# Scattering eight raw fields of an edge instead of a full row of 143 values, in a graph network of four layers

## The chip, the cores and the metric

The kernel runs on one core of a Trainium2 chip. The time is that of the whole program on the device, in microseconds. A run of the profiler takes one execution apart; times inside it are counted from the start of its span. The engines are named as in the profile: PE multiplies matrices (PEld loads its weights), DVE is the vector engine, ACT the scalar engine, POOL the general engine that also issues the indirect transfers, and SP only issues transfers. Each works through its own queue of instructions in order.

## The reference, cut to what matters

A graph of 3,125 nodes with 32 features and 103,125 edges (50,000 pairs in both directions and one loop per node). Four layers are added to the features one after the other: attention with four heads, a mean over neighbours in two steps, a Gaussian mixture, and a spline convolution on positions that a small network with two further spline convolutions moves. The part that the change touches belongs to the edges: every edge has its two ends and five attributes. Three of these are a position `pseudo` in [0, 1], from which the splines take a cell and weights:

```python
def spline_basis(pseudo):
    pos = pseudo * (KS - 1)
    i0 = jnp.clip(jnp.floor(pos), 0, KS - 2).astype(jnp.int32)
    frac = pos - i0
    basis = jnp.prod(jnp.where(combos[None] == 1, frac[:, None, :], 1.0 - frac[:, None, :]), axis=-1)
    idx = jnp.sum((i0[:, None, :] + combos[None]) * strides[None, None, :], axis=-1)
    return (basis, idx)

def spline_conv(x, row, col, basis, idx, W, b):
    z = jnp.einsum('ni,kio->nko', x, W).reshape(N * K, Fout)
    gathered = z[col[:, None] * K + idx]
    msg = jnp.einsum('es,eso->eo', basis, gathered)
    out = jax.ops.segment_sum(msg, row, num_segments=N)
    deg = jax.ops.segment_sum(jnp.ones_like(msg[:, 0]), row, num_segments=N)
    return out / jnp.maximum(deg, 1.0)[:, None] + b
```

with KS = 5, so 125 kernel positions and 8 corners per edge. For the first of the spline convolutions the input feature is 1 for every node, so only the sums of the 125 basis values over the edges of a node are needed.

## The kernel before

**Stages.** The nodes are held in 25 chunks of 128. The work goes through these stages, with their times in the profiled execution:

- *Places* (0 to 132 us, `places_of_edges`). For each edge the place in a table is found: edges with the same source chunk are packed into tiles of 128, 855 tiles in all. Eight fields of an edge (low part of the source, target, three Gaussian weights, three position values) are collected in `flds`, field by field, and stored to `fields_d` (L1036 to L1144).
- *Scatter* (132 to 1,832 us, L1544 to L1706). `put_edges` (L1564) takes 26 columns of 128 edges at a time: SP loads their fields (L1567), DVE computes cells, the eight corner weights and all 125 basis values into `pay` (L1570 to L1593, three buffers), and POOL sends 26 indirect transfers (L1595), each of 128 rows of 143 values (`ROW` = 17 + 125 + 1; 572 bytes) into the table `tab` in device memory. There are 31 such blocks, 806 transfers. Rows that may remain empty are filled by transfers on ACT's queue first (L1562).
- Inside the scatter stage the tiles are read back by groups. A group is 2 to 5 units of 24 tiles (one tile per full source chunk), and five small groups of 3 tiles hold the last chunk. `add_tiles` (L1623) loads the rows of three source chunks at a time (L1637, on SP), copies the ends (DVE, L1643) and the 17 narrow values (ACT, L1646), and then goes source chunk by source chunk: DVE makes one-hots of the source (L1650, helper L1374), PE multiplies them with the 126 wide values of the rows (L1653), and the sum is added to `sums` (L1608). For groups that come early enough (`counted`) the same step also counts edges between nodes: ACT casts the one-hots (L1657), DVE makes one-hots of the targets (`od`, L1381), PE multiplies (L1496), DVE or ACT takes the counts on (L1520, L1522), and `counts_out` (L1530) stores the counts, their transpose and a third array, `off`, which is 0 where an edge exists and very large elsewhere (ACT, L1534; `a_off` has one buffer).
- *Spline convolution 2* (1,832 to about 3,760 us). Per chunk PE computes the table `z` (L1445), ACT and DVE copy it to slabs, ACT's queue stores them. `summed_rows` (L1708) then gathers, tile by tile (POOL, L1731), multiplies by corner weights (DVE, L1735) and sums with one-hots (PE, L1736). The corner weights of a group come into `w8` (L1890). Beside it, in portions that `beside` deals out, run the remaining counts and the maximum of the attention scores (L1836 to L1843): SP loads `off` for each source chunk and third of the targets, and DVE runs one subtract-and-maximum per head (L1841).
- *Attention* (to 4,685), the mean, the mixture and the new positions (to 5,755), and the *last spline convolution* (5,755 to 7,187), which has the same shape as the earlier one at half the width, with 12 gather buffers, three buffers for `prod` and two for the one-hots `oh2`.

**The order.** The order of the program around the scatter is written by hand: after each block, steps of the groups whose tiles are complete are put in, two blocks late (`LAG`, L1683 to L1697), so that they spread over the blocks until the next group comes. A group can be read when the blocks up to its `need` have been scattered: 71, 155, 292, 425, 557, 689, 768, 806 and 806 columns for the nine large groups. The last three large groups (72, 96 and 72 tiles) and two small ones are worked off after the last block (L1699 to L1705), two at a time in turn. What reads `tab` has been declared independent of the scatters of later blocks (L1639), so only the scatters of earlier blocks are waited for.

Of the kernel before, what the change touches and what calls it, by code (L numbers as in the profile page):

```python
# [8 lines left out]
F32 = mybir.dt.float32  # L9
BF = mybir.dt.bfloat16  # L10
I32 = mybir.dt.int32
I16 = mybir.dt.int16
AF = mybir.ActivationFunctionType
OP = mybir.AluOpType
# [4 lines left out]
P = 128  # L19
# [855 lines left out]
ROW = NAR + K3 + 1  # L875
# [101 lines left out]
def places_of_edges(tc, a, pl, tr, fields_d, slot_d):  # L977
# [12 lines left out]
    with tc.tile_pool(name="bk", bufs=1) as pool:  # L990
# [45 lines left out]
        flds = pool.tile([P, 8, tr], F32, name="flds")  # L1036
# [107 lines left out]
        nc.sync.dma_start(fields_d, flds.rearrange("p f t -> p (f t)"))  # L1144
# [42 lines left out]
def cells(nc, pool, pos, n):  # L1187

    cell = pool.tile([P, 3, n], F32, name="cell")
    tmp = pool.tile([P, 3, n], F32, name="cell_t")  # L1190
    nc.vector.tensor_scalar(cell, pos, 1.0, None, op0=OP.is_ge)
    for k in range(2, KS - 1):
        nc.vector.tensor_scalar(tmp, pos, float(k), None, op0=OP.is_ge)
        nc.vector.tensor_add(cell, cell, tmp)
    hat = pool.tile([P, 3, 2, n], F32, name="hat")
    nc.vector.tensor_sub(hat[:, :, 1, :], pos, cell)
    nc.vector.tensor_scalar(hat[:, :, 0, :], hat[:, :, 1, :], -1.0, 1.0, op0=OP.mult, op1=OP.add)
    return cell, hat


def corner_weights(nc, pool, cell, hat, n, w8, row):

    w4 = pool.tile([P, 2, 2, n], F32, name="w4")
    nc.vector.tensor_mul(w4, hat[:, 1, :, None, :].to_broadcast([P, 2, 2, n]),
                         hat[:, 2, None, :, :].to_broadcast([P, 2, 2, n]))
    nc.vector.tensor_mul(w8, w4.rearrange("p j k t -> p (j k) t")[:, :, None, :].to_broadcast([P, 4, 2, n]),
                         hat[:, 0, None, :, :].to_broadcast([P, 4, 2, n]))
    tmp = pool.tile([P, n], F32, name="cell_row")
    nc.vector.scalar_tensor_tensor(tmp, cell[:, 0], float(KS), cell[:, 1], op0=OP.mult, op1=OP.add)
    nc.vector.scalar_tensor_tensor(row, tmp, float(KS), cell[:, 2], op0=OP.mult, op1=OP.add)  # L1210
# [3 lines left out]
def tile_gnn_places(ctx: ExitStack, tc: tile.TileContext, a: dict, out: bass.AP, pl, fields_d, slot_d):  # L1214
# [34 lines left out]
    big = const.tile([P, 1], F32, name="big")  # L1249
    nc.vector.memset(big, BIG)  # L1250
# [60 lines left out]
    off_d = [dram.tile([P, NPAD], BF, name=f"off_d{s}") for s in range(NCH)]  # L1311
# [170 lines left out]
    def count_edges(g, s, oh, cps, tps):  # L1482
# [9 lines left out]
        for i, (t, w) in enumerate(tiles):  # L1492
            od = cn_a.tile([P, 9 * P], BF, name="od3", bufs=4)
# [9 lines left out]
    def add_counts(s, cols, cn, tps):  # L1503

        lo, width = cols[0][0], len(cols)
        a_s = cn_a.tile([P, 8 * P], F16, name="a_s")
# [23 lines left out]
    def counts_out(s, lo, n, a_s, tps):  # L1530

        nc.sync.dma_start(as_d[s][:, lo * P : (lo + n) * P], a_s[:, : n * P])
        off = cn_a.tile([P, 8 * P], BF, name="a_off", bufs=1)
        nc.scalar.activation(off[:, : n * P], a_s[:, : n * P], AF.Relu, bias=big, scale=-BIG)  # L1534
        nc.sync.dma_start(off_d[s][:, lo * P : (lo + n) * P], off[:, : n * P])
        a_t = cn_a.tile([P, 8 * P], F16, name="a_t")
# [7 lines left out]
    SB = 3  # L1544
    assert S % SB == 0
    GK = max(len(g.units) for g in pl.groups)
    GT = max(g.n for g in pl.groups)
    with tc.tile_pool(name="ed", bufs=1) as once, tc.tile_pool(name="ed_pay", bufs=3) as pays, \
            tc.tile_pool(name="ed_s", bufs=2) as small_p, tc.tile_pool(name="s1", bufs=2) as pool, \
# [5 lines left out]
        EM = 5  # L1555
# [8 lines left out]
        def put_edges(t0):  # L1564
            n = BLK
            at = small_p.tile([P, 8, BLK], F32, name="flds", bufs=3)
            nc.sync.dma_start(at, fields_d.rearrange("p (f t) -> p f t", f=8)[:, :, t0 : t0 + n])  # L1567
            pay = pays.tile([P, BLK, ROW], F32, name="pay")
            pos = small_p.tile([P, 3, BLK], F32, name="pos")
            nc.vector.tensor_scalar(pos, at[:, 5:8], float(KS - 1), None, op0=OP.mult)  # L1570
            cell, hat = cells(nc, small_p, pos, n)
            nc.vector.tensor_copy(pay[:, :, 0:8].rearrange("p t f -> p f t"), at)
            corner_weights(nc, small_p, cell, hat, n, pay[:, :, 9:17].rearrange("p t (c i) -> p c i t", i=2), pay[:, :, 8])
            w15 = small_p.tile([P, 3, KS, BLK], F32, name="w15")
            tmp = small_p.tile([P, 3, BLK], F32, name="w15_t")
            for k in range(KS):
                if k < KS - 1:
                    nc.vector.scalar_tensor_tensor(w15[:, :, k, :], cell, float(k), hat[:, :, 0, :],
                                                   op0=OP.is_equal, op1=OP.mult)
                if k:  # L1580
                    dest = tmp if k < KS - 1 else w15[:, :, k, :]
                    nc.vector.scalar_tensor_tensor(dest, cell, float(k - 1), hat[:, :, 1, :],
                                                   op0=OP.is_equal, op1=OP.mult)
                    if k < KS - 1:
                        nc.vector.tensor_add(w15[:, :, k, :], w15[:, :, k, :], tmp)
            w25 = small_p.tile([P, KS, KS, BLK], F32, name="w25")
            nc.vector.tensor_mul(w25, w15[:, 0, :, None, :].to_broadcast([P, KS, KS, n]),
                                 w15[:, 1, None, :, :].to_broadcast([P, KS, KS, n]))
            nc.vector.tensor_mul(
                pay[:, :, NAR : NAR + K3].rearrange("p t (i k) -> p i k t", k=KS),  # L1590
                w25.rearrange("p i j t -> p (i j) t")[:, :, None, :].to_broadcast([P, KS * KS, KS, n]),
                w15[:, 2, None, :, :].to_broadcast([P, KS * KS, KS, n]))
            nc.vector.memset(pay[:, :, ROW - 1 :], 1.0)  # L1593
            for k in range(n):
                put = nc.gpsimd.indirect_dma_start(  # L1595
                    out=tab, out_offset=bass.IndirectOffsetOnAxis(ap=slot[:, t0 + k : t0 + k + 1], axis=0),
                    in_=pay[:, k, :], in_offset=None, bounds_check=P * NT - 1, oob_is_err=False)
# [3 lines left out]
                tc.add_to_no_dep_group(f"rows{t0}", put.ins)  # L1601

# [20 lines left out]
        def add_tiles(g, nar, m, s0, ns):  # L1623

            t0, off = g.t0, s0 if ns == SB else 0
            tt = pool.tile([P, GK, SB, ROW], F32, name="tt")
            if ns == SB:
                src = tabv[:, t0 : t0 + g.n, :].rearrange("e (k s) f -> e k (s f)", s=S)[:, :, s0 * ROW : (s0 + ns) * ROW]
                mine = tt[:, :m, :, :]
                into = mine.rearrange("p k s f -> p k (s f)")  # L1630
                spread = lambda v: v.rearrange("p f (k s) -> p f k s", s=S)[:, :, :, s0 : s0 + ns]
            else:
                src = tabv[:, t0 : t0 + m, :].rearrange("e k f -> e (k f)")
                into = tt.rearrange("p k s f -> p (k s f)")[:, : m * ROW]
                mine = into.rearrange("p (k s f) -> p k s f", s=1, f=ROW)
                spread = lambda v: v.rearrange("p f (k s) -> p f k s", s=1)
            got = nc.sync.dma_start(into, src)  # L1637
# [3 lines left out]
            low = spread(ends[:, :, t0 : t0 + g.n])  # L1641
            for f in range(2):
                nc.vector.tensor_copy(low[:, f], mine[:, :, :, f])  # L1643
            nv = spread(nar[:, :, : g.n])
            for k in range(m):
                nc.scalar.copy(nv[:, :, k, :].rearrange("p f s -> p s f"), mine[:, k, :, :NAR])  # L1646
            for i in range(ns):
                s = g.units[0].tiles[s0 + i][0] if ns == SB else S
                oh = pool.tile([P, GK, P], F32, name="oh1")
                onehots(oh, iota_f, low[:, 0, :, i], m)  # L1650
                acc = psa.tile([P, 512], F32, name="acc1")
                for k in range(m):
                    nc.tensor.matmul(acc[:, : K3 + 1], oh[:, k, :], mine[:, k, i, NAR:], start=(k == 0), stop=(k == m - 1))  # L1653
                counts = None
                if g.counted:
                    ohb = cn_a.tile([P, GK, P], BF, name="oh3")
                    nc.scalar.copy(ohb[:, :m], oh[:, :m])  # L1657
# [3 lines left out]

        def group_steps(g):
            n = g.n
            nar = pool.tile([P, NAR, GT], F32, name="nar", bufs=2)
            if g.t0 < pl.tail:
                for s0 in range(0, S, SB):
                    yield from add_tiles(g, nar, len(g.units), s0, SB)
            else:
                yield from add_tiles(g, nar, n, 0, 1)
            nc.sync.dma_start(narrow_d[g.t0].rearrange("p (f t) -> p f t", f=NAR), nar[:, :, :n])  # L1670
            table_rows(pool, g.t0, n, nar[:, 8, :n], GT)
            for q0 in range(0, n, P):
                q = min(P, n - q0)
                lt = pst.tile([P, 2, P], F32, name="lt")
                for i, (row_d, dt) in enumerate(((lorow_d, BF), (dstrow_d, I16))):
                    nc.tensor.transpose(lt[:q, i, :], ends[:, i, g.t0 + q0 : g.t0 + q0 + q], ident)
                    lr = pool.tile([P, P], dt, name=f"lr{i}")
                    nc.scalar.copy(lr[:q], lt[:q, i, :])
                    nc.sync.dma_start(row_d[g.t0 + q0 : g.t0 + q0 + q], lr[:q])
# [4 lines left out]
        todo = [[g.need + LAG * BLK, (S if g.t0 < pl.tail else 1) + 1, group_steps(g)] for g in pl.groups]  # L1684
# [23 lines left out]
    def summed_rows(grp, fout, table, w8_of, total, first, pool, gp, pp, psa, beside=None):  # L1708
# [14 lines left out]
        for s, tiles in grp.sources.items():  # L1723
            n = len(tiles)
            oh = pool.tile([P, GK, P], F32, name="oh2")
# [530 lines left out]
```

## Time and profile before

| | us |
|---|---|
| median of 3 runs | 7,230.65 |
| lowest, highest | 7,201.02, 7,293.86 |
| the profiled execution | 7,211.97 |
| its span | 7,210.2 |

| engine | busy us | share of the span |
|---|---|---|
| PE | 4,521.4 | 63% |
| DVE | 4,517.0 | 63% |
| POOL | 2,847.0 | 39% |
| PEld | 2,281.7 | 32% |
| ACT | 1,673.9 | 23% |

No engine is full over the whole; each stage has its own limit. The page draws that as 40 slices of 180 us, each digit the busy share of a slice in tenths:

```profile
DVE  5334355533575757877798889917998945444444
POOL 0777544460242534565574000000000035567776
DMA  2123344425787987897883434361114478755553
```

The scatter stage is slices 2 to 10 (from the left), with DVE at half and POOL at 4 to 7 tenths; the first spline convolution is slices 11 to 21, where the transfers and DVE come near full; the last one is slices 32 to 40.

The groups of instructions that the change removes, moves or doubles read as follows (busy us and mean ns of one, then the idle time before them and what ended it):

```profile
L1595 POOL DMA_INDIRECT tab<-pay,slot x806 | 884.7, 1098 | 590.0 <-issue 241.1 <-DVE od L1381 180.9 <-DVE a_s L1520 63.6
L1589 DVE TENSOR_TENSOR pay<-w,w 128x3250 f32<-128x3250 f32 x31 | 176.5, 5694 | 2.3 <-DVE cell L1194 1.1 <-DVE cell_t L1193 1.1
L1841 DVE CUSTOM_DVE_ANT_0 junk<-adr,off 128x1024 f32<-128x1024 f32 (+1 forms) x300 | 379.0, 1263 | 40.3 <-ACT adr L1835 38.3
L1534 ACT ACTIVATE a_off<-a_s,big 128x384 bf16<-128x384 f16 (+4 forms) x219 | 131.9, 602 | 294.8 <-DMA off_d<-a_off 139.4 <-DVE a_s L1520 89.5 <-issue 29.0
```

### The profile page before, as it was taken

The numbers are of one execution on the slowest core, as the hardware profiler recorded it, in microseconds if no ns is written. First come the engines' busy times: TensorE is split into PE (matmuls) and PEld (weight loads), VectorE is DVE, ScalarE is ACT, GpSimd is POOL, SyncE is SP. The second block draws the span as 40 slices with busy tenths as digits, with TensorE's granted clock in tenths as the row PEclk, the third lists the DMA queues.
The fourth block names the chain that finished last, engine by engine and source line by source line (L and its number), as shares of the span: only waits on it lengthen the run. The fifth ranks groups of instructions, "written<-read, shape, count | busy, mean of one in ns | idle before, by whom it ended". The sixth has DMA issues, their size and how long they took to land. (4 is left out here: it accounts for less than half of the span.)

```text
span 7210.2 us, 68160 instructions
## 1 busy us (share of the span) xinstructions
PE 4521.4 (63%) x20874; PEld 2281.7 (32%) x20904; DVE 4517.0 (63%) x9289; ACT 1673.9 (23%) x2940; POOL 2847.0 (39%) x2543
## 2 busy tenths in 40 slices
PE   4013244415888878887778877766775489855555
PEld 1012133214332323222222322255664433333333
DVE  5334355533575757877798889917998945444444
ACT  0012133201434232221103778801110012100000
POOL 0777544460242534565574000000000035567776
PEclk5555566657888977788788999976885556566666
DMA  2123344425787987897883434361114478755553
GB/s 97 53 81 97 86 122 121 124 81 135 265 305 266 335 301 269 322 352 267 291 282 108 119 115 126 101 227 53 57 56 161 160 247 297 237 155 157 159 156 82
DMA packets 554782, 1265.69 MB, mean 176 GB/s; under 512 B 273204, under 2 KB 363263, under 8 KB 541478
## 3 DMA queue, kind: packets, MB, share of 16 engines
q0 software_dynamic: 148912, 613.60, 25.7%
q1 hardware_dynamic: 359062, 388.16, 18.3%
q10 hardware_dynamic: 46432, 259.48, 9.2%
q8 instruction: 168, 2.75, 0.2%
q14 instruction: 208, 1.70, 0.1%
HBM read 907.51 MB, written 387.39 MB: 180 GB/s over the span
## 5 line engine op out<-in xcount | busy, mean ns | idle before, releaser
L1731 POOL DMA_INDIRECT g<-z,base x1710 | 1950.1, 1140 | 1741.9 <-DVE prod L1735 421.8
L1736 PE MATMUL acc<-prod,oh 128*128 128x512 f32 (+1 forms) x3420 | 1690.3, 623 | 733.6 <-DVE prod L1735 506.3
L1736 PEld LDWEIGHTS acc<-prod,oh 128*128 128x128 f32 x3420 | 719.1, 237 | 1663.1 <-issue 828.9
L1595 POOL DMA_INDIRECT tab<-pay,slot x806 | 884.7, 1098 | 590.0 <-issue 241.1
L1374 DVE TENSOR_TENSOR oh<-iota_f,ends 128x640 f32<-128x640 f32 (+3 forms) x663 | 444.5, 672 | 693.7 <-remote 409.8
L1381 DVE TENSOR_SCALAR od<-iota_n,ends 128x512 bf16<-128x512 int16 (+5 forms) x1721 | 536.0, 357 | 495.0 <-remote 207.2
L2189 POOL MEMSET g<- 128x448 f32 x5 | 2.1, 474 | 1876.5 <-PE t_ps L2162 1876.5
L1653 PE MATMUL acc<-tt,oh 128*128 128x126 f32 x1710 | 337.7, 359 | 612.3 <-DVE od L1381 248.5
L1735 DVE TENSOR_TENSOR prod<-g,w 128x512 f32<-128x512 f32 x855 | 579.1, 686 | 211.2 <-DMA g<-z,base 183.5
L1997 PE MATMUL acc<-wt,hx 128*33 128x416 f32 (+1 forms) x1600 | 587.8, 516 | 142.6 <-DVE wt L1995 126.5
L1445 PE MATMUL z_ps<-wk,hts 64*128 64x512 f32 (+1 forms) x800 | 479.9, 845 | 65.6 <-ACT slab L1459 36.2
L1653 PEld LDWEIGHTS acc<-tt,oh 128*128 128x128 f32 x1710 | 302.7, 261 | 650.3 <-issue 427.4
L1496 PE MATMUL cn<-od,oh 128*128 128x256 bf16 (+3 forms) x1331 | 304.7, 358 | 234.4 <-DVE od L1381 107.3
L1841 DVE CUSTOM_DVE_ANT_0 junk<-adr,off 128x1024 f32<-128x1024 f32 (+1 forms) x300 | 379.0, 1263 | 40.3 <-ACT adr L1835 38.3
L1459 ACT COPY slab<-z_ps 128x512 f32<-128x512 f32 (+11 forms) x575 | 289.8, 516 | 486.3 <-DVE slab L1457 309.2
L1735 DVE TENSOR_TENSOR prod<-g,w8n 128x256 f32<-128x256 f32 x855 | 333.5, 423 | 107.0 <-PE acc L1736 49.0
L1991 DVE SCALAR_TENSOR_TENSOR low<-rows,bias_d,low 128x1664 f32<-128x1664 f32 (+1 forms) x200 | 369.4, 1882 | 9.5 <-ACT low L1990 9.5
L1995 DVE SCALAR_TENSOR_TENSOR wt<-low,cnt 128x1664 f32<-128x1664 f32 (+1 forms) x200 | 357.5, 1818 | 15.2 <-PE acc L1997 6.8
L1990 ACT ACTIVATE low<-rows,bias_d 128x1664 f32<-128x1664 f32 (+1 forms) x200 | 325.1, 1628 | 133.4 <-DVE wt L1995 103.0
L1997 PEld LDWEIGHTS acc<-wt,hx 128*33 128x33 f32 x1600 | 168.5, 113 | 527.5 <-issue 334.9
L1993 ACT ACTIVATE low<-low 128x1664 f32<-128x1664 f32 (+1 forms) x200 | 307.0, 1537 | 104.4 <-DVE low L1991 104.3
L1539 PE MATMUL cn<-ident_h,a_s 128*128 128x128 f16 x625 | 98.3, 257 | 336.1 <-DVE a_s L1520 142.7
(348 smaller groups left out, 5211.5 us busy)
## 6 DMA issues: line engine op xcount, KB each, us to landing
z<-slab ACTq DMA_DIRECT2D x100, 1600.0 KB
z<-slab ACTq DMA_DIRECT2D x100, 800.0 KB
lob<-lorow_d SPq DMA_DIRECT2D x70, 768.0 KB
cnt<-at_d SPq DMA_DIRECT2D x100, 416.0 KB
cnt<-as_d SPq DMA_DIRECT2D x50, 800.0 KB
cnt<-at_d SPq DMA_DIRECT2D x100, 384.0 KB
tt<-tab SPq DMA_DIRECT2D x32, 1072.5 KB
g<-z,base POOLq DMA_INDIRECT x1710
```

What stands on the lines that cost most here:

```text
L1374: nc.vector.tensor_tensor(dst_tile[:, :n, :], iota[:, None, :].to_broadcast([P, n, P]), lows[:, :, None].to_broadcast([P, n, P]), OP.is_equal)
L1381: nc.vector.tensor_scalar(dst_tile[:, :w], iota_n[:, lo * P : lo * P + w], ends[:, 1, t : t + 1], None, op0=OP.is_equal)
L1445: nc.tensor.matmul(ps[:, k - k0 : k - k0 + n, :].rearrange("p r f -> p (r f)"), vt[g * fin : (g + 1) * fin, :], wk[g * fin : (g + 1) * fin ...
L1595: put = nc.gpsimd.indirect_dma_start(out=tab, out_offset=bass.IndirectOffsetOnAxis(ap=slot[:, t0 + k : t0 + k + 1], axis=0), in_=pay[:, k, ...
L1653: nc.tensor.matmul(acc[:, : K3 + 1], oh[:, k, :], mine[:, k, i, NAR:], start=(k == 0), stop=(k == m - 1))
L1731: nc.gpsimd.indirect_dma_start(out=g, out_offset=None, in_=table[:rows], in_offset=bass.IndirectOffsetOnAxis(ap=base[:, t : t + 1], axis=0 ...
L1735: nc.vector.tensor_mul(prod, corners(g, fout), w8_of(t).to_broadcast([P, 2, 4, fout]))
L1736: nc.tensor.matmul(acc, oh[:, i, :], prod.rearrange("p j c f -> p (j c f)"), start=(i == 0), stop=(i == n - 1))
L1841: nc.vector.tensor_tensor_reduce(junk, adr[:, hd, :], off, 1.0, -BIG, OP.subtract, OP.max, top[:, j, s, hd : hd + 1])
L1991: nc.vector.scalar_tensor_tensor(low, rows[0], bias_d[:, 0, d, hd : hd + 1], low, op0=OP.add, op1=OP.max)
L1995: nc.vector.scalar_tensor_tensor(wt, low, 1.0, cnt, op0=OP.min, op1=OP.mult)
L1997: nc.tensor.matmul(acc[:, i, :q], hx[:, d, :], wt[:, i * q : (i + 1) * q], start=(d == 0), stop=(d == NCH - 1))
```

## The change

The row of an edge in the table is cut to the eight raw fields, 32 bytes (`ROW` = 8). `places_of_edges` stores the fields edge by edge instead of field by field. `put_edges` only issues the scatters, straight from the fields, which are loaded once in two halves. Cells, corner weights and the one-dimensional weights `w15` are computed after a group has been read back, for all its tiles at once; the 125 basis values are computed for each step (the tiles of one source chunk in the group), by `basis`, into one of three buffers whose last column is 1. The load of a group is one transfer. The first step of a group is these computations alone, so a group has one step more than before.

The array `off` is no longer stored. The attention part loads the counts and makes the flag on DVE, in f32, one instruction for each source chunk and third of the targets (75 in all).

Numbers of buffers change in several places: the pool of the scatter steps 2 to 3 and its small tiles 2 to 1; `od3` 4 to 3, `a_s` 2 to 4, `a_t` 2 to 3; `oh2` 2 to 3; `prod` 3 to 4 in the first spline convolution and 3 to 8 in the last; `w8` 2 to 1. Empty rows are filled 48 tiles at a time instead of 5.

The core of the diff (`cells` and `corner_weights` compute as before, with room for the largest group):

```diff
-ROW = NAR + K3 + 1
+ROW = 8
...
-        flds = pool.tile([P, 8, tr], F32, name="flds")
+        flds_e = pool.tile([P, tr, ROW], F32, name="flds")
+        flds = flds_e.rearrange("p t f -> p f t")
...
-        nc.sync.dma_start(fields_d, flds.rearrange("p f t -> p (f t)"))
+        nc.sync.dma_start(fields_d, flds_e.rearrange("p t f -> p (t f)"))
...
-        off = cn_a.tile([P, 8 * P], BF, name="a_off", bufs=1)
-        nc.scalar.activation(off[:, : n * P], a_s[:, : n * P], AF.Relu, bias=big, scale=-BIG)
-        nc.sync.dma_start(off_d[s][:, lo * P : (lo + n) * P], off[:, : n * P])
-        a_t = cn_a.tile([P, 8 * P], F16, name="a_t")
+        a_t = cn_a.tile([P, 8 * P], F16, name="a_t", bufs=3)
...
+        flds = once.tile([P, tr, ROW], F32, name="e_flds")
+        fv = fields_d.rearrange("p (t f) -> p t f", f=ROW)
+        for t0 in range(0, tr, tr // 2):
+            nc.sync.dma_start(flds[:, t0 : t0 + tr // 2, :], fv[:, t0 : t0 + tr // 2, :])
+        EM = 48
...
         def put_edges(t0):
...
-            for k in range(n):
+            for t in range(t0, t0 + BLK):
                 put = nc.gpsimd.indirect_dma_start(
-                    out=tab, out_offset=bass.IndirectOffsetOnAxis(ap=slot[:, t0 + k : t0 + k + 1], axis=0),
-                    in_=pay[:, k, :], in_offset=None, bounds_check=P * NT - 1, oob_is_err=False)
+                    out=tab, out_offset=bass.IndirectOffsetOnAxis(ap=slot[:, t : t + 1], axis=0),
+                    in_=flds[:, t, :], in_offset=None, bounds_check=P * NT - 1, oob_is_err=False)
...
+        spread = [once.tile([P, GK, K3 + 1], F32, name=f"basis{i}") for i in range(3)]
+        def basis(w15, tiles, m):
+            b = spread[at_step[0] % len(spread)]
+            at_step[0] += 1
+            w25 = pool.tile([P, KS, KS, GK], F32, name="w25")
+            nc.vector.tensor_mul(w25[:, :, :, :m], w15[:, 0, :, None, tiles].to_broadcast([P, KS, KS, m]),
+                                 w15[:, 1, None, :, tiles].to_broadcast([P, KS, KS, m]))
+            nc.vector.tensor_mul(
+                b[:, :m, :K3].rearrange("p t (i k) -> p i k t", k=KS),
+                w25[:, :, :, :m].rearrange("p i j t -> p (i j) t")[:, :, None, :].to_broadcast([P, KS * KS, KS, m]),
+                w15[:, 2, None, :, tiles].to_broadcast([P, KS * KS, KS, m]))
+            return b
...
+        def group_steps(g):
+            n, m, t0 = g.n, len(g.units), g.t0
+            regular = t0 < pl.tail
+            tt = group_p.tile([P, GT, ROW], F32, name="tt")
+            got = nc.sync.dma_start(tt[:, :n, :], tabv[:, t0 : t0 + n, :])
...
+            nc.vector.tensor_copy(ends[:, :, t0 : t0 + n].rearrange("p f t -> p t f"), tt[:, :n, :2])
+            nar = group_p.tile([P, NAR, GT], F32, name="nar")
+            nc.scalar.copy(nar[:, :8, :n].rearrange("p f t -> p t f"), tt[:, :n, :])
+            pos = small_p.tile([P, 3, GT], F32, name="pos")[:, :, :n]
+            nc.vector.tensor_scalar(pos, nar[:, 5:8, :n], float(KS - 1), None, op0=OP.mult)
+            cell, hat = cells(nc, small_p, pos, n, GT)
+            corner_weights(nc, small_p, cell, hat, n, nar[:, 9:17, :n].rearrange("p (c i) t -> p c i t", i=2), nar[:, 8, :n], GT)
+            w15 = group_p.tile([P, 3, KS, GT], F32, name="w15")
...
+            yield
+            for i in range(S if regular else 1):
...
                 oh = pool.tile([P, GK, P], F32, name="oh1")
-                onehots(oh, iota_f, low[:, 0, :, i], m)
+                onehots(oh, iota_f, ends[:, 0, t0 : t0 + n][:, tiles], count)
+                b = basis(w15, tiles, count)
                 acc = psa.tile([P, 512], F32, name="acc1")
-                for k in range(m):
-                    nc.tensor.matmul(acc[:, : K3 + 1], oh[:, k, :], mine[:, k, i, NAR:], start=(k == 0), stop=(k == m - 1))
+                for k in range(count):
+                    nc.tensor.matmul(acc[:, : K3 + 1], oh[:, k, :], b[:, k, :], start=(k == 0), stop=(k == count - 1))
...
-                    off = pool.tile([P, w], BF, name="off")
-                    nc.sync.dma_start(off, off_d[s][:, c0 * P : c0 * P + w])
+                    cnt = pool.tile([P, w], F16, name="cnt")
+                    nc.sync.dma_start(cnt, as_d[s][:, c0 * P : c0 * P + w])
+                    off = pool.tile([P, w], F32, name="off", bufs=1)
+                    nc.vector.tensor_scalar(off, cnt, 0.0, BIG, op0=OP.is_equal, op1=OP.mult)
...
-                w8 = pool.tile([P, 8, GT], F32, name="w8")
+                w8 = pool.tile([P, 8, GT], F32, name="w8", bufs=1)
```

## The prediction

> **What bounds the kernel now.** I read the busy time by stage first (the windows view), then who holds the scatter back (waits of POOL and DVE), then the timeline of one scatter, then the later stages that the change also touches. Columns of the windows: stretch, its length, busy time of PE, PEld, DVE, ACT, POOL (instructions), granted clock, DMA share, GB/s.
>
> ```profile
> 132.00:173.00 41.00, 0.00 (x0) 0.00 (x0) 17.79 (x60) 0.00 (x0) 4.36 (x8) 0.50 0.83 263
> 173.00:1612.00 1439.00, 392.08 (x2084) 288.04 (x2098) 601.04 (x1726) 281.14 (x804) 884.70 (x806) 0.58 0.35 95
> 1612.00:1832.00 220.00, 120.87 (x687) 110.96 (x687) 92.05 (x330) 23.14 (x125) 3.99 (x5) 0.73 0.54 135
> 2750.00:3740.00 990.00, 776.59 (x1368) 251.16 (x1368) 790.82 (x1403) 177.94 (x427) 567.78 (x442) 0.81 0.83 299
> 6300.00:7187.00 887.00, 455.55 (x1211) 289.33 (x1210) 395.81 (x1041) 0.00 (x0) 629.43 (x607) 0.69 0.52 145
> ```
>
> The scatter stage (173 to 1612) is the one where no engine is full: DVE is busy 42%, PE 27%, POOL 61%. Everything in it is paced by POOL, which sends 806 scatters, and the last groups (1612 to 1832) can only start when the last scatter has landed. So the question is what POOL waits for:
>
> ```profile
> POOL tab L1595 <- issue: 241.1, 786, 1.7
> POOL tab L1595 <- DVE od L1381: 180.9, 6, 46.0
> POOL tab L1595 <- DVE a_s L1520: 63.6, 3, 33.9
> POOL tab L1595 <- DVE pay L1589: 49.2, 1, 49.2
> ...
> DVE od L1381 <- remote: 207.2, 47, 26.0
> DVE pay L1572 <- DMA tab<-pay,slot: 182.4, 9, 27.3
> DVE oh L1374 <- remote: 145.0, 21, 15.0
> ```
>
> The first line is the fixed gap of 0.30 us between two scatters. The others are waits of some 20 to 49 us: the payload of the next 26 tiles is made by DVE, and DVE stands in its own queue behind a group's one-hots, which wait for loads and for PE. The second half shows DVE waiting for scatters in turn (three payload buffers). Two queues in order, each waiting for the other. The timeline shows the rest:
>
> ```profile
> 605.69 0.97 POOL L1595 DMA_INDIRECT tab<-pay,slot  x1 [0.30 <-issue]
> 606.38 5.68 DVE L1589 TENSOR_TENSOR pay<-w,w 128x3250 f32<-128x3250 f32 x1
> 606.97 5.83 POOL L1595 DMA_INDIRECT tab<-pay,slot  x1 [0.30 <-issue]
> 613.10 0.97 POOL L1595 DMA_INDIRECT tab<-pay,slot  x1 [0.30 <-issue]
> ```
>
> A free scatter takes 0.97 + 0.30 = 1.28 us. One that starts under a long two-input DVE instruction is held until that ends.
>
> **The change, part by part.** The sum is made against the profiled execution (7,212.0 us, span 7,210.2); the median of the runs shown is 7,230.65, 0.26% above it.
>
> *First 173 us.* Eight ACT copies and exponentials write the fields at a step of 32 B, two DVE instructions read them so. The row for such an ACT pass is 0.94 us (q2, 128x806); doubling would add 8 us, nothing would add 0. I take +3.
>
> *Scatter.* Removed from DVE ahead of each 26 scatters: the payload, 31 times one 5.69 us instruction, one of 0.83 and some 25 of 0.2 us. Removed from SP: 31 field loads; two halves of 1.6 MB come instead, which at the 263 GB/s of the first row take 6 us each. ACT's queue has 4 fills of empty rows instead of 25. POOL's scatters then wait for nothing but slots, first half and fills. First scatter near 165. Pace: 806 x 1.275 = 1,028 us. Add what DVE still holds up. Before, the mean scatter is 1,098 ns against 974 free: 806 x 0.124 = 100 us, nearly all from some twenty holds of 5 us. Afterwards the holders are 147 products of up to 625 elements (the groups that run beside the scatter), some 1.2 us each, and the one-hots (0.82 us). A hold costs what is left of it when a scatter starts: 147 x 0.4 = 59 us plus about 40 for one-hots, 100 again. Bounds: 0, and 147 x 1.4 + 60 = 266 if every such instruction stops POOL wholly.
>
> [...]
>
> So the last scatter is near 165 + 1,028 + 100 = 1,293 instead of 1,612.
>
> *Are the group steps fast enough?* They get DVE's payload work back. Per step: the product (L1589 rate 5,694/3,250 = 1.75 ns an element, the output stepping some 500 B as before), 625 elements, 1.1 us; the 125-element product 0.2 us; with one-hot 0.75, five targets of 0.29, carry add 0.5, sum 0.2 a counted step of five tiles is 4.2 us of DVE, 24 of them 101 us, plus some 27 small instructions a group (0.2 to 0.5 us, 10 us). Such a group comes every 132 tiles, 132 x 1.38 = 182 us. It fits, with waits in it. If the stepped inputs (96 B) cost as much again the product is 1.6 us, and it still fits. The load of a group is one (120 tiles x 32 B a partition) instead of eight of 1 MB; it waits on SP for the scatters of its tiles, and behind it stand the count stores of the step before, whose tiles now have 4 and 3 buffers, so ACT and PE do not feel it. od3 goes from 4 to 3: DVE waited 41 us there for PE in this stage, hidden now that POOL does not wait for DVE; uncovered it would cost some tens of us.
>
> *Last groups (220 us before).* There DVE waited 88.3 us for loads of tt. Now 72 steps on DVE: three tiles 0.47 + 0.15 + 0.64 + 0.20 = 1.46 us, four 1.83; 24 x (2 x 1.46 + 1.83) = 114, three group starts 24, the two small groups 10: 150 us, DVE-bound, PE's 121 beside it. Stage end 1,293 + 150 = 1,443 against 1,832, -389. I leave 17 us for steps still open when the scatter ends: **-372**.
>
> *Flags in the spline stage (to 3,740).* ACT loses 219 activations of 0.60 us and their stores; they waited 139.4 us for the store of the one before. 100 of them lie in 1,832 to 2,750, where ACT is 37% busy: take -15 (0 to -60). DVE gains 75 instructions turning counts (mean 1,066 elements) into flags. Not in the trace; nearest row, the f32 TENSOR_SCALAR over 806 elements, 0.58 us: 0.65 to 0.77 us each, 50 to 58 in all; at the one-element rate of L1841 (1.22 us) 92. Between 2,750 and 3,740 DVE is 80% busy, and back to back at the end. I take +40 (0 to +95). w8 has one buffer: its load on SP waits for the last product of the group before, behind it wait the count loads (4 buffers), and DVE's first product waits for it. A small load took 6 us from issue to use (152.5 to 158.5); 13 changes give at most 78, only three of them back to back: +15. More buffers for prod and oh2: DVE waited 19 + 19 us for PE here: -10. Sum **+30**.
>
> *Last stage.* oh2 3, prod 8 buffers. In 6,300 to 7,187 DVE's one-hots waited 118.1 us and products 44.6 for PE, but 249.4 more for gathers to land, and POOL's floor is 607 x 1.30 = 789 of 887 us. So 0 to -98; nearest the low end, since the landing decides: **-20**.
>
> Sum: 3 - 372 + 30 - 20 = -359, 6,853 for the profiled execution, x 1.0026 = **6,870 us** as a median.
>
> **Rivals.** (a) *The group chain becomes the bound.* DVE waited some 560 us in the scatter stage for things marked remote, issue and PE; if these belong to the steps themselves, they stay. Its 601 us less some 300 of payload leave 300 of group work; with 200 of basis and 560 of waits that makes 1,060, under 1,280, but badly placed waits push the end to some 1,640: -190 there, about 7,060. For it: counted groups arrive in bursts (two blocks for 26 steps). Against it: many waits were for 1 MB loads. 10%.
>
> (b) *POOL isn't freed.* The waits for od and a_s are inferred; were they room in POOL's descriptor ring or landing writes, only the last groups gain (-70) and +30 remains: 7,190, no change. Against it: the waits come once every 26 scatters, just where a payload starts. 8%.
>
> (c) *Slower: 32-byte rows.* [...] In 180 to 360 us 122 scatters of 572-byte rows take a DMA share of 0.17: 0.17 x 180 x 16 / (122 x 128) = 31 ns a row. [...] It would decide from 0.16 us a row, and make the kernel slower by 2% from 0.256 us (2.05 us a scatter). At 0.3 us, 2.4 x 806 = 1,934 us, the stage ends at 2,249: about 7,640. 8%.
>
> **The numbers.** The likely case has 74% (own range 6,740 to 7,000: the holds 0 to 266, flags 0 to +95, buffers 0 to -98). Range 6,740 to 7,080: it takes in rival (a) and leaves out (b), (c) and a little below. A measurement tells 2% here, 7,086 to 7,375. Faster 0.83 (the likely case and most of (a)), same 0.09, slower 0.08.
>
> **What would show it.** Right: POOL's waits for DVE gone between scatters, last scatter near 1,290, no 5 us scatters, tt loads of 32-byte rows, z work from about 1,440, DVE some 50 us fuller before the attention stage. Wrong: scatters of over 1.5 us with DMA waits (c), waits of the same length in POOL (b), or DVE steps running on long after the last scatter (a); gaps of several us at w8 would say that the one buffer costs more.

## The result and the profile after

The changed kernel is 1% slower: 7,317.8 us against 7,242.6 us (medians of 13 runs each on one chip), ratio 1.010, 95% interval 1.0077 to 1.0122. The forecast was 6,870 us. The profiled execution took 7,304.9 us, its span is 7,303.1, 92.9 us more than that of before. By stages, from the first instruction of one to that of the next:

| | before | after | difference | forecast |
|---|---|---|---|---|
| first to last scatter | 173 to 1,611 | 161 to 1,248 | 362 earlier | 318 earlier |
| first slab of the spline stage | 1,834 | 1,973 | +139 | -372 |
| from there to the first `wt` of attention | 1,951 | 1,937 | -14 | +30 |
| from there to the first gather of the last stage | 2,028 | 2,010 | -18 | 0 |
| from there to the last product | 1,385 | 1,372 | -13 | -20 |

Everything that went wrong lies between the last scatter and the first slab. Before, 224 us passed there; now it is 724. The other stages differ by 13 to 18 us, which is no more than the same code differs from run to run in the experiments below. The windows view of the changed kernel, cut at the last scatter (stretch, length, busy PE, PEld, DVE, ACT, POOL with instructions, granted clock, DMA share, GB/s):

```profile
173.00:1250.00 1077.00, 92.17 (x351) 58.44 (x352) 101.87 (x309) 49.00 (x172) 827.89 (x797) 0.50 0.05 8
1250.00:1973.00 723.00, 444.63 (x2445) 330.11 (x2451) 653.68 (x1604) 156.45 (x362) 4.48 (x5) 0.75 0.18 41
```

POOL is free, as forecast: 77% busy, the rest being the gaps between scatters. But beside it nothing runs. DVE is 9% busy, PE 9%, the transfers 5%, and of the 221 steps that make a basis only 41 are done. The other 180 stand behind the last scatter, where DVE is 90% busy. What the steps wait for beside the scatter (waits view, 132 to 1,973 us: us in total, times, longest):

```profile
ACT a_t L1536 <- remote: 564.2, 28, 29.9
DVE od L1380 <- remote: 535.9, 58, 23.4
PE cn L1495 <- issue: 516.7, 43, 28.4
...
POOL tab L1564 <- issue: 251.4, 805, 0.8
```

POOL's waits for DVE are gone; only the 0.3 us between scatters is left. In their place stand waits with no visible releaser: "remote" and "issue" mean that the profile finds no event that ended them. The timeline of one counted step shows whose they are:

```profile
599.78 0.27 ACT L1521 CAST a_s<-cn 128x128 f16<-128x128 f32 x1
...
600.11 0.29 PE L1535 MATMUL cn<-ident_h,a_s 128*128 128x128 f16 x1 [4.60 <-ACT a_t L1536]
...
600.87 1.06 PE L1649 MATMUL acc<-basis,oh 128*128 128x126 f32 x4
...
603.12 0.32 DVE L1380 TENSOR_SCALAR od<-iota_n,ends 128x384 bf16<-128x384 int16 x1 [5.45 <-PE acc L1649]
...
603.49 0.48 PE L1495 MATMUL cn<-od,oh 128*128 128x384 bf16 x1 [1.56 <-issue]
...
615.72 0.29 DVE L1380 TENSOR_SCALAR od<-iota_n,ends 128x256 bf16<-128x256 int16 x1 [11.79 <-remote]
...
619.22 0.27 ACT L1536 COPY a_t<-cn 128x128 f16<-128x128 f16 x1 [18.59 <-remote]
...
619.87 0.29 PE L1535 MATMUL cn<-ident_h,a_s 128*128 128x128 f16 x1 [15.90 <-issue]
```

Follow one tile. ACT's cast `a_s` ends at 600.05, and PE starts to transpose it at 600.11: what ACT and DVE hand to PE arrives at once (0.06 us after this cast; 0.05 from the end of `od` at 603.44 to the product at 603.49). The transpose is one instruction of 0.29 us by the record. Its copy `a_t` starts at 619.22, 18.8 us later, though nothing stands before it on ACT. The same holds for `od` on DVE, which waits for PE to free a buffer. What waits for PE is released 3 to 19 us late, and only that. The records show when PE's instructions start, their ends are modelled, so they don't tell whether PE itself works slowly or its signal comes late; below it is called a late release. A step of two tiles has a period of 19.6 us (599.62 to 619.22 for `a_t`), and the releases come mostly in multiples of 0.70 us: 603.12 to 615.72 is 18 of them, 615.72 to 619.22 five, and from there to the next `od` at 622.02 four.

Behind the last scatter (1,248.47) this lasts for some 25 us more, then it is over. DVE in the timeline:

```profile
1268.51 0.32 DVE L1380 TENSOR_SCALAR od<-iota_n,ends 128x384 bf16<-128x384 int16 x1 [16.52 <-remote]
1271.31 0.32 DVE L1380 TENSOR_SCALAR od<-iota_n,ends 128x384 bf16<-128x384 int16 x1 [2.48 <-remote]
...
1279.47 0.55 DVE L1373 TENSOR_TENSOR oh<-iota_f,ends 128x384 f32<-128x384 f32 x1
...
1282.87 0.55 DVE L1373 TENSOR_TENSOR oh<-iota_f,ends 128x384 f32<-128x384 f32 x1
```

From 1,279 us on a counted step of three tiles takes 3.40 us (1279.47 to 1282.87). Beside the scatters such a step of three tiles had taken 30.8 us, as the copies show that end two of them:

```profile
1154.86 0.37 ACT L1536 COPY a_t<-cn 128x256 f16<-128x256 f16 x1 [29.77 <-remote]
...
1185.68 0.37 ACT L1536 COPY a_t<-cn 128x256 f16<-128x256 f16 x1 [29.77 <-remote]
```

Same code, same buffers, a ninth of the time.

POOL pays as well. Its scatters come every 1.28 us until 616 us and every 1.40 on average from there:

```profile
614.82 0.97 POOL L1564 DMA_INDIRECT tab<-e_flds,slot  x1 [0.30 <-issue]
616.09 1.30 POOL L1564 DMA_INDIRECT tab<-e_flds,slot  x1 [0.30 <-issue]
...
621.64 1.10 POOL L1564 DMA_INDIRECT tab<-e_flds,slot  x1 [0.30 <-issue]
```

It had been there before the change. The timeline of the kernel before, in a run of scatters without a pause:

```profile
443.12 1.19 PE L1653 MATMUL acc<-tt,oh 128*128 128x126 f32 x4 [7.24 <-DVE ends L1643]
...
450.75 1.06 PE L1653 MATMUL acc<-tt,oh 128*128 128x126 f32 x4
```

```profile
449.51 0.27 ACT L1611 COPY sums<-acc 128x126 f32<-128x126 f32 x1 [6.16 <-remote]
...
460.00 0.26 ACT L1611 COPY sums<-acc 128x126 f32<-128x126 f32 x1 [9.61 <-remote]
```

By the modelled ends the sums are made at 444.3 and 451.8; they are copied at 449.5 and 460.0, 5 and 8 us late. But there POOL stopped for its next payload again and again. The "remote" waits of more than 4 us on ACT and DVE lie where it did not stop: in them a scatter went out every 1.41 us, over the whole scatter every 1.79. That the steps caught up in the pauses is a reading of this, not a test.

### The profile page after: what moved, and what is told of

The parts are those of the page before. It is cut to its first block, busy times and chain, and to the rows that moved or that the text cites. A ratio compares the mean times of both kernels' runs of the same rounds, so it can differ in the third digit from the quotient of the medians.

```text
span 7303.1 us, 65789 instructions
## 1 busy us (share of the span) xinstructions
PE 4505.2 (62%) x20880; PEld 2252.2 (31%) x20904; DVE 4596.3 (63%) x9153; ACT 1532.1 (21%) x2440; POOL 2830.1 (39%) x2543
## 5 line engine op out<-in xcount | busy, mean ns | idle before, releaser
L1718 POOL DMA_INDIRECT g<-z,base x1710 | 1980.1, 1158 | 1473.9 <-DVE prod L1722 420.6
L1723 PE MATMUL acc<-prod,oh 128*128 128x512 f32 (+1 forms) x3420 | 1662.2, 615 | 747.9 <-DVE prod L1722 470.2
L1564 POOL DMA_INDIRECT tab<-e_flds,slot x806 | 837.4, 1039 | 271.5 <-issue 251.4
L1649 PE MATMUL acc<-basis,oh 128*128 128x126 f32 x1710 | 335.1, 359 | 181.1 <-DVE basis L1585 157.3
L1495 PEld LDWEIGHTS <-oh 128*128 128x128 bf16 x1359 | 143.7, 112 | 728.9 <-issue 579.1
L1649 PEld LDWEIGHTS acc<-basis,oh 128*128 128x128 f32 x1710 | 291.7, 257 | 239.1 <-DVE basis L1585 199.9
```

What stands on the lines that cost most here:

```text
L1495: nc.tensor.matmul(cn[:, b, at : at + n], oh[:, i, :], od[:, f : f + n], start=(i == spans[b][0]), stop=(i == spans[b][1]), skip_group_che ...
L1564: put = nc.gpsimd.indirect_dma_start(out=tab, out_offset=bass.IndirectOffsetOnAxis(ap=slot[:, t : t + 1], axis=0), in_=flds[:, t, :], in_o ...
L1649: nc.tensor.matmul(acc[:, : K3 + 1], oh[:, k, :], b[:, k, :], start=(k == 0), stop=(k == count - 1))
L1718: nc.gpsimd.indirect_dma_start(out=g, out_offset=None, in_=table[:rows], in_offset=bass.IndirectOffsetOnAxis(ap=base[:, t : t + 1], axis=0 ...
L1723: nc.tensor.matmul(acc, oh[:, i, :], prod.rearrange("p j c f -> p (j c f)"), start=(i == 0), stop=(i == n - 1))
```

## The experiments

Theory 1: while POOL issues scatters back to back, what waits for PE is released late, and spaces between the scatters cure it. Theory 2: the steps are slow by their own chain of waits and few buffers, whatever POOL does. All edits are to the changed kernel where nothing else is said. The first four ran on one chip, where the kernel before took 7,170.2 us (one run), the others on a second, where its median was 7,180.8 and not 7,242.6. The changed kernel itself was not run beside them, so some 60 us of a difference from its 7,317.8 can be the chip's. The run with one memset in 13 scatters, which behaves as the changed kernel does, stands in for it on the second chip.

**Spaces between the scatters.** A memset of POOL (128 x 256) behind each:

```diff
                 tc.add_to_no_dep_group(f"rows{t0}", put.ins)
+                nc.gpsimd.memset(idle, 0.0)
```

> A POOL memset of 256 columns (some 0.3 us) follows each of the 806 scatters of the changed kernel, so that 100 us hold some 60 scatters instead of 72 to 79. Theory 1 (while POOL issues scatters back to back, what waits for PE is released late; spaces between scatters cure it): last scatter near 1,500 instead of 1,250, but a counted step then takes some 5 us during the scatter instead of 19.6, few steps are left at the end, the spline stage's first slab comes near 1,680 instead of 1,973, total some 7,030. Theory 2 (the steps are slow by their own chain of waits and few buffers, whatever POOL does): still some 19.6 us a step, the same pile behind a later end, first slab near 2,150, total some 7,480.

7,108.3 us in one run, beside 7,170.2 of the kernel before. Last scatter 1,479, first slab 1,733, 126 of 221 steps done by the last scatter. That is 50 to 80 us above what theory 1 expected and some 370 to 420 below theory 2, which is out: chain and buffers are unchanged. The order of the instructions is not quite: in the queue of DVE the first 365 are the same, then some are exchanged. But the 365th starts at 553 us here and at 1,297 in the changed kernel, so the gain is there before the order differs. Not one wait for "remote" is left in this stage's waits view, and a counted step of three tiles takes 3.4 us beside the scatters:

```profile
501.34 0.54 DVE L1373 TENSOR_TENSOR oh<-iota_f,ends 128x384 f32<-128x384 f32 x1
...
504.76 0.54 DVE L1373 TENSOR_TENSOR oh<-iota_f,ends 128x384 f32<-128x384 f32 x1
```

The same 100 us by windows, changed kernel first, then with spaces:

```profile
500.00:600.00 100.00, 9.75 (x35) 5.44 (x35) 8.40 (x25) 6.64 (x29) 76.21 (x79) 0.50 0.05 7
```

```profile
500.00:600.00 100.00, 41.03 (x180) 30.05 (x178) 46.56 (x128) 18.71 (x49) 89.54 (x128) 0.50 0.12 25
```

Five times the matmuls at the same granted clock of 0.50, so it is not the clock that PE lacked. POOL's timeline shows how small the space is:

```profile
500.94 0.97 POOL L1565 DMA_INDIRECT tab<-e_flds,slot  x1 [0.17 <-issue]
501.90 0.34 POOL L1572 MEMSET idle<- 128x256 f32 x1
502.41 1.47 POOL L1565 DMA_INDIRECT tab<-e_flds,slot  x1 [0.16 <-issue]
```

The memset lies in what was a gap of 0.30 us. A scatter that nothing holds comes every 1.46 instead of 1.28 us. Once steps run beside it, DVE's holds (the 1.47 us scatter) bring the mean to 1.53 to 1.85.

**The same time in pauses.** 26 memsets in a row behind each block of 26 scatters:

```diff
+            for t in range(BLK):
+                nc.gpsimd.memset(idle, 0.0)
```

> The same 806 memsets, but 26 of them in a row behind each block of 26 scatters: the same POOL time, one pause of some 9 us a block. If it is the space between two scatters that PE needs, steps stay slow within the blocks and only the pauses help: some 10 to 20 more steps done by the last scatter (near 1,500), first slab near 2,050, total some 7,400. If a pause is as good as a space (theory 1 in its wide form), as with spaced scatters: first slab near 1,680, total some 7,030. Theory 2: near 2,150, total 7,480.

7,118.1 us, first slab 1,734. The run doesn't answer its question: when the program was put in order, the memsets were spread between the scatters, one each, so that it repeats the first experiment (7,108.3) and shows how well that repeats. A pause kept in one piece was not tried.

**No step beside the scatters.**

```diff
-        LAG = 2
+        LAG = 40
```

> No group step is put in beside the scatters: all come behind the last one (lag of 40 blocks instead of 2). Scatters unhindered: last one near 1,200. Then the steps run at the pace seen behind the scatter, some 730 us of DVE in all (412 + 217 + 100 busy in the stage of the changed kernel): first slab near 1,950 to 2,000, total 7,300 to 7,350, so that the steps beside the scatter brought nothing. If the steps beside the scatter were worth their number (about 55 of some 220), it would come some 150 us later, 7,470.

7,365.8 us, last scatter 1,190, first slab 1,992. The total is 16 us above the range expected. The 41 steps beside the scatter had won some 20 us at the first slab, net of the 58 us by which they made the last scatter later. The run also gives the other half of the contention. With PE, DVE and ACT at rest beside them, all 806 scatters take 974 ns and come every 1.28 us:

```profile
L1564 POOL DMA_INDIRECT tab<-e_flds,slot x806 | 784.9, 974 | 266.1 <-issue 245.4 <-DMA e_flds<-fields_d 20.6
```

So the fall to 1.40 needs the steps. It needs something more as well: in the changed kernel steps ran beside the scatters from 340 us on, and the pace fell only at 616. What, stays open.

**A busy POOL without indirect transfers.** 1,600 memsets in a row behind the last scatter:

```diff
+        for i in range(1600):
+            nc.gpsimd.memset(idle, 0.0)
         rest = [steps for *_, steps in todo]
```

> POOL runs 1,600 memsets without a pause from the last scatter on, while the remaining steps run (some 560 us at 0.35 us each). If it is the issue of indirect transfers that holds PE's results back, the steps behind the scatter stay at 4 to 5 us: first slab within 30 us of 1,973, total 7,290 to 7,350 (first gathers come after 2,070, behind the memsets). If any busy POOL does it, the steps go on at some 19.6 us until the memsets end: first slab near 2,450, total near 7,800.

7,549.0 us, first slab 2,295: neither figure. The windows view says why that total must not be read as slow steps. The changed kernel, then this one:

```profile
1250.00:1800.00 550.00, 334.31 (x1933) 239.56 (x1938) 494.88 (x1144) 152.58 (x347) 0.84 (x1) 0.77 0.20 47
```

```profile
1250.00:1800.00 550.00, 333.49 (x1819) 232.91 (x1820) 490.29 (x1053) 151.43 (x346) 451.12 (x1390) 0.77 0.20 46
```

With POOL 82% busy with memsets, PE and DVE do as much as without. The total is longer because with a POOL booked until then the program was ordered anew: 767 target one-hots came before the first slab instead of 489, counts that otherwise run beside the spline stage. So a POOL that is busy with memsets alone does nothing, and the late releases go with its indirect transfers.

**The smallest space.** One column (128 x 1) instead of 256, kept in its place:

```diff
+                tc.keep_in_program_order(put)
+                tc.keep_in_program_order(nc.gpsimd.memset(idle, 0.0))
```

> A memset of one column (some 0.1 us) follows each scatter, kept in its place. In the run with 256 columns the memset took the place of the 0.30 us gap (0.17 of it stayed), so here the pace should stay at 1.24 to 1.28 us, 78 to 80 scatters in 100 us, as dense as in the changed kernel. If the slow PE comes from indirect instructions of POOL that follow one another with no other POOL instruction between: no late releases, last scatter near 1,200, stage end DVE-bound some 200 to 350 us after it, first slab near 1,500 to 1,600, total 6,880 to 6,990. If it comes from the density of scatters in time (over some 70 in 100 us): late releases as in the changed kernel, first slab near 1,970, total some 7,310.

7,068.5 us against 7,180.8 of the kernel before: ratio 0.984, interval 0.978 to 0.989, so it is faster than the kernel before by measurement, and by the ratios (0.984 against 1.010) than the changed kernel. Last scatter 1,339, first slab 1,707, between the two expectations. The order of the program is ruled out here as a cause: up to the first slab DVE and ACT run the same 1,913 and 533 instructions in the same order as in the changed kernel. The mean pace is 1.40 to 1.44 us until 800 us, slower than I had reckoned, and late releases are shorter, not gone (waits view; the two lines give 7 us a wait, where those of the changed kernel gave 13):

```profile
ACT a_t L1537 <- remote: 284.0, 25, 19.4
...
DVE od L1381 <- remote: 224.2, 47, 17.1
```

Another POOL instruction between two scatters is therefore not what cures; with one at every place, half of the waiting stays. By the mean pace of 100 us the runs line up roughly: at 1.28 to 1.41 us releases come up to some 28 us late, here at 1.40 to 1.45 mostly under 14, and in stretches above 1.5 (here from 900 to 1,000 and from 1,100 to 1,300, and with 256 columns while steps run) `a_t` and `od` wait for "remote" not once. That is no threshold. Where steps run, DVE's holds slow the scatters too, so part of the slower pace comes from the cure; and in the run that follows, 500 to 700 us have a mean of 1.47 to 1.50 with waits of up to 18.6 us.

**One memset in 13 scatters.** `if t % 13 == 12:` ahead of the memset.

> The one-column memset after every 13th scatter only. If each run of indirect instructions starts anew after a memset and PE becomes slow only some way into it, steps are faster than in the changed kernel but not as fast as with one memset per scatter: first slab between 1,600 and 1,900, total 7,000 to 7,250. If only the scatters themselves count, as the changed kernel: 7,310. If any memset now and then is enough: as with one per scatter.

7,286.2 us in one run, first slab 1,956, 47 steps by the last scatter, `a_t` waiting 614 us for "remote". As the changed kernel: a rare POOL instruction does nothing. DVE and ACT again run the same instructions in the same order, so the 249 us between this first slab and the 1,707 above, on the same chip, belong to the memset behind every scatter.

**The kernel before, with the one-column memset.**

> The kernel before, with the one-column memset after each of its scatters. Its steps waited 207 + 145 us for things marked remote, too. If those waits are the same thing: they go, POOL waits less for DVE (180.9 + 63.6 us before), last scatter some 150 to 300 us earlier than 1,611, total 6,950 to 7,100. If they are something else (loads of 1 MB, the payload chain): same within 30 us of the kernel before.

7,178.6 us against 7,180.8, ratio 1.000, interval 0.997 to 1.004; last scatter 1,607. The "remote" waits went from 224 + 207 + 145 us for `a_t`, `od` and `oh` to 141 + 141 + 147, and nothing came of it. In that kernel something else sets POOL's pauses; but as three quarters of this waiting stayed (429 of 576 us), it doesn't show what it cost there.

**The memset behind the 1,710 gathers as well.**

> As the run with one-column memsets after scatters, and one after each of the 1,710 gathers of the two spline convolutions as well. In the last stage, where 67 to 69 gathers go out in 100 us, some releases by PE came 3 to 6 us late. If these cost time there: last stage 30 to 100 us shorter than in the run with memsets after scatters only. If the gathers' own pace decides (1.30 us each, which the memset may even shorten to 1.26): within 30 us of it.

7,053.8 us, ratio to the kernel before 0.986, interval 0.980 to 0.992, not to be told from the run without it. From the first gather of the last stage to the last product the profiled execution takes 1,358 us instead of 1,396, inside the 30 to 100 us expected, but the same code took 1,372 to 1,406 in the other runs without these memsets, so one profiled execution does not show a gain. The one-hots still wait 236 us for "remote" (239 without), and the gathers still come every 1.31 us: no space was made that could help.

## Why the prediction was wrong

**The step that failed** is "Are the group steps fast enough?", in the phrase "It fits, with waits in it". I added up DVE's busy time (4.2 us for a counted step of five tiles) and put the waits at nothing. A step of two tiles took 19.6 us, and not for DVE's sake, so that 41 of 221 steps were done by the last scatter and 724 us followed it, not 167. The waits were in the profile of before: `a_t` and `od` waited 224 and 207 us for "remote", up to 30 us at a time, with a releaser that no view named.

```profile
ACT a_t L1540 <- remote: 224.1, 23, 30.2
```

I put many of them down to loads of 1 MB, which rival (a) lists as evidence against itself. A look at their place would have shown PE's work done and its taker waiting, in the lines at 443 to 460 us above. The other phrase of that step, that more buffers keep the count stores from ACT and PE, held: neither `a_t` nor `a_s` waits for a store in this stage.

**Rival (a)** is what happened: the group chain became the bound. I gave it 10% and 7,060 us. Its price assumed that the waits of before would stay as they were. They grew when the change took POOL's pauses away: before, 33 to 75 scatters went out in each 100 us from 200 to 1,600 us; after, 71 to 78 from 200 to 1,200. That space between the scatters shortens the waits is shown for the changed kernel (256 columns, one column); that the pauses kept them short before is the likely reading.

**Places and scatter** came out. First scatter at 161 (forecast 165), POOL's waits for DVE gone, last scatter at 1,248 (1,293). It was earlier because what lengthened the scatters took 52 us, 806 x (1,039 - 974) ns, instead of 100 by DVE's holds alone. Half of the 52, some 26 us, lies in scatters beside which DVE did nothing, which is the new pace; DVE hardly ran. With DVE at work the term is about right: with spaces the mean scatter is 1,130 ns, 126 us over 806, and with no DVE at all it is 974 to the nanosecond. So it was right to go by the row at 606.97, where a scatter took 5.83 us under a long product: the scatter at 502.41 takes 1.47 us, and it starts under the 0.82 us product of 502.20; those at 500.94 and 504.37, clear of one, take 0.97.

**Last groups: mis-sized.** Forecast were 150 us behind the last scatter and 17 for open steps. With spaces it is 253 (1,480 to 1,733), DVE 93% busy. The groups view of that stretch, DVE by form:

```profile
L1587 DVE TENSOR_TENSOR basis<-w,w 128x375 f32<-128x375 f32 x50 | 41.1, 822 | 0.0
L1587 DVE TENSOR_TENSOR basis<-w,w 128x625 f32<-128x625 f32 x21 | 34.7, 1650 | 0.0
L1587 DVE TENSOR_TENSOR basis<-w,w 128x500 f32<-128x500 f32 x24 | 27.7, 1155 | 0.0
```

Three tiles: 0.55 one-hot, 0.28, 0.82 product, 0.28 sum = 1.93 us, not 1.46; four tiles 2.48, not 1.83. That is 24 x (2 x 1.93 + 2.48) = 152 instead of 114. And 21 steps of five tiles, some 66 us, were still open when the last scatter went. The product takes 2.2 to 2.6 ns an element, not 1.75. Its inputs step as well as its output, a case that I had only as an upper bound (1.6 us for 625 elements; 1.65 came); that the step is the reason was not tested.

How the forecast first slab (1,834 - 372 = 1,462) becomes 1,733 with spaces: 186 us from the later last scatter (1,479 instead of 1,293; about 806 x 0.18 = 145 of it is the memsets), 86 from the longer tail (253 instead of 167). From there to the 1,973 of the changed kernel, 240 us, is what the late releases cost on top of the price of the cure; between the two runs on one chip (one memset in 13 scatters, one column behind each), with half of the waiting still there in the better one, it is 249 (1,956 and 1,707).

**Flags, buffers.** The flags cost what was worked out: 75 instructions of 693 ns, 52 us. The stage became 14 us shorter, not 30 longer. Its second part, where they run (DVE 861 us busy instead of 822), took 1,033 us instead of 1,026, the first 904 instead of 925. But with the changed code for this stage the first part took 895 to 930 us and the second 1,022 to 1,040 in the runs above (leaving out the busy POOL, which moved counts out of it), and the kernel before with its memset took 911 and 1,030. So the flags lie mostly beside other work; a relief by `a_off`, `prod` or `oh2` is not shown. Nor is one in the last stage: 13 us less in one profiled execution of each, where the same code took 1,372 to 1,406.

**Rivals (b) and (c)** are out: POOL was freed, and rows of 32 bytes are scattered every 1.28 us as those of 572 were. From 300 to 1,200 us the queue of the indirect transfers took 2.8% of the 16 engines' time for 663 scatters, 0.028 x 900 x 16 / (663 x 128) = 4.8 ns a row; rows of 572 bytes took 28 (15.0% for 122 scatters, 180 to 360 us). (c) would have decided from 160 ns (1.28 us over 8 rows, 128 by 16 engines).

## What to carry to other kernels

A wait whose releaser the profile can't name is a cost of unknown cause, not spare time: look up its place in the timeline, find whose result was ready, and ask what will happen to it when the engine beside it stops pausing. Removing one engine's stalls makes it a denser neighbour (33 to 75 scatters in 100 us before, 71 to 78 after); here 0.18 us more from scatter to scatter took 240 us out of the stage. When a long stretch shows one engine busy and everything else idle with no named releaser, try thinning that engine out before touching the chain that waits.

## What was not expected of the hardware

Steps that wait for PE and a POOL that issues indirect transfers back to back slow each other down: releases by PE mostly in steps of 0.70 us and up to some 28 us late, scatters from 1.28 to 1.40 us, with the transfers 5% busy and the granted clock unchanged at 0.50. The slow scatters start two such steps apart (1,239.37, 1,240.77, 1,242.17); whether that is chance was not tested. It outlasts the last scatter by some 25 us (1,248 to 1,275). Waits of the same kind stand in the last stage too, where gathers come every 1.30 us and `oh` waits 265 us (before) and 285 us (after) for "remote"; that they have the same cause is not shown. The cause stays open: no run here shows what lies between PE and POOL. It isn't the clock (0.50 with spaces and without, from 500 to 600 us), POOL being busy with memsets (82% of 550 us, with the same work of PE and DVE), the size of the rows (late releases at 572 bytes, by 5 and 8 us, and at 32), the steps' buffers or the order of the program (both unchanged in the run with one column behind each scatter, where `a_t` waited 284 us for "remote" instead of 564).
